# A graph network on one NeuronCore: first products before the second graph's inputs, a re-listed last chain, the last output block through SBUF

## The chip, the cores and the metric

The kernel runs on one core of a Trainium2 chip. The time is what the device measures for one launch, in microseconds (us); of several runs the median counts. All arithmetic is in float32. TensorE (PE) multiplies matrices, VectorE (DVE), ScalarE (ACT) and GpSimd (POOL) do the elementwise work, and SyncE (SP) issues the transfers between the chip's memory and the on-chip memory SBUF. Matrix products land in PSUM, which here is used as eight banks of 128 x 512 numbers.

## What is computed

There are 64 graphs of 256 nodes with 512 features each, and one adjacency matrix `adj` (256 x 256) for all. Two layers follow each other, both with a residual connection. The normalisation has no learned scale.

```python
h = relu(layernorm(x))                                  # layer 0: attention with a mask
q, k, v = h @ Wq + bq, h @ Wk + bk, h @ Wv + bv         # 8 heads of 64
p = softmax(q @ k.T / 8 + (1 - adj) * -1e9)             # per graph and head
x = x + (p @ v) @ Wo + bo

h = relu(layernorm(x))                                  # layer 1: graph attention
g = h @ W
s1, s2 = g @ a1, g @ a2
e = leaky_relu(s1[:, None] + s2[None, :], 0.2) * adj
x = x + elu(softmax(e) @ g + beta * g)
```

## The kernel before

**Pairs and seven products.** The graphs are worked off in 32 pairs. For a pair, the activations form a 2 x 2 matrix of blocks: the rows are the two graphs, the columns the two halves of 256 features. Each weight matrix is split 2 x 2 as well. A product of the two is then made with seven block products in place of eight. This needs four sums of blocks on each side ahead of the products and seven sums of results behind them. `Unit.p(i)` (L261-275) issues product i, where i is 1 to 7; each product is eight matmuls of 128 x 256. `UnitQK` makes q and k (two units, `ua` and `ub`, of one 128-column tile each), `UnitV`, `UnitO` and `UnitW` make v, the output projection and the second layer's product. Products 1 and 2 need only original blocks, products 5 to 7 and 3 need sums. The activation's sums are `combine_31` (L281), `combine_2` and `combine_4` (L291, L295). Weight sums are made once by `weight()` (L101-121). The sums of results are in the `put...` functions of each unit: `put11` after product 2, `put2` (`put2_sums` and `put2_elu` in `UnitW`) after product 5, `put12` after product 3. The block that a product writes into is taken from eight PSUM banks in turn, and the elementwise tiles from pools with a fixed number of buffers per tag (`set`, `qk`, `v`, `pt`, `xt`, ...).

**Layer 0.** `load(p)` (L76) fetches x of a pair. `stats` and `scales` (L231-248) make mean and reciprocal deviation on DVE and POOL. ACT normalises x in place, `x_t` (L307) transposes it on TensorE and ACT applies relu (h). `combine_31` of h reads the transposes of the second graph straight from PSUM. `scores` (L396) makes q.k, exp on ACT and the mask on POOL; `values` (L425) makes p.v, and the division on DVE gives `oT`. `o_blocks` (L439) forms the first two sums of oT on POOL. `residual` (L449) loads x once more and adds the bias on POOL.

**Layer 1.** `normal` (L490) makes the normalised h of this layer on ACT; `node_sums` (L493, called by `y_sums`) makes s1 and s2 as weighted row sums on DVE (tile `pr`). `gat_scores` (L499) spreads s2 along the rows with two small transposes (tile `pe`) and makes e on DVE, `gat_exp` the exponential on ACT, `gat_divide` (L515) the division with beta added on DVE, `gat_t` (L523) the transposes (tile `at`) and an ACT copy (`eT`). `z_graph` (L532) multiplies h by that, 16 matmuls a graph (tile `pz`), and copies the result with ACT to `z`. `UnitW` (L560) is the last product; `elu` (L566) makes relu and exp of the negative part on ACT and max(x, 0) + y on DVE, `finish` (L575) adds both on POOL and issues the output transfer. For the very last block `put12_finish` (L601) does this in two halves of 256 columns.

**Order.** The order of the instructions on TensorE, DVE, ACT and POOL is the order in which the Python code issues them (`tc.manual_schedule`, L969). Each of these engines works its list off from front to back; an instruction whose inputs are not there holds up all behind it. SP's list of transfers is arranged by the framework. `start()` (L675) is the beginning of the first pair, the loop body is `first_half` and `second_half`, which interleave the two layers of neighbouring pairs, `last()` (L859) is the last pair's layer 0, and `end()` (L910) the second layer of the last two pairs, 60/61 and 62/63. Behind `end()` comes a check (L991-1003) that the softmax sums lie in a safe range: seven small DVE operations, a matmul `count`, and a flag. The flag decides whether a second, slower version of the program has to be run; SP loads it and branches.

Of the kernel before, what the change touches and what calls it, by code (L numbers as in the profile page):

```python
# [23 lines left out]
def kernel(ctx: ExitStack, tc: tile.TileContext, x, adj, wq, bq, wk, bk, wv, bv, wo, bo, w, a, beta, out):  # L24
# [42 lines left out]
    def two(ps):  # L67
        return ps.rearrange("p (j n) -> p j n", j=2)
# [7 lines left out]
    def load(p):  # L76
        for g in (2 * p, 2 * p + 1):
            for t in range(NT):
                XT[g, t] = sb([P, D], "xt", f"x_{g}_{t}", BUFS["xt"])
                nc.sync.dma_start(XT[g, t], x[g, t * P:(t + 1) * P, :])  # L80

    load(0)
# [18 lines left out]
    def weight(name, src, permuted=False):  # L101

        raw = const.tile([P, 3, 2, N], F32, name=f"{name}_b")
        b12 = blk("set", f"{name}_b12")
        tt = const.tile([P, 4, 2, N], F32, name=f"{name}_t")
        for dst, r, f in ((raw[:, 0], 0, 0), (raw[:, 1], 1, 0), (b12, 0, 1), (raw[:, 2], 1, 1)):
            if permuted:
                for i in range(4):
                    nc.sync.dma_start(dst[i * HH:(i + 1) * HH], wo_rows(src)[r, i, :, :, f * N:(f + 1) * N])
            else:  # L110
                nc.sync.dma_start(dst, rows_in_order(src)[r, :, :, f * N:(f + 1) * N])
        b11, b21, b22 = (raw[:, i] for i in range(3))
        t1, t2, t3, t4 = (tt[:, i] for i in range(4))

        def sums():
            nc.vector.tensor_tensor(t1, b12, b11, ALU.subtract)
            nc.vector.tensor_tensor(t2, b22, t1, ALU.subtract)
            nc.vector.tensor_tensor(t3, b12, b22, ALU.subtract)
            nc.vector.tensor_tensor(t4, b21, t2, ALU.subtract)

        return {1: b11, 2: b21, 3: b22, 4: t4, 5: t1, 6: t2, 7: t3}, b12, sums
# [7 lines left out]
    WQ, _, wq_sums = weight("wq", wq)  # L129
    WK, _, wk_sums = weight("wk", wk)  # L130
# [4 lines left out]
    WV, _, wv_sums = weight("wv", wv)  # L135
# [26 lines left out]
    def project_b():  # L162


        WO, b12, sums = weight("wo", wo, True)
        nc.sync.dma_start(bo2, bo.partition_broadcast(P))
        bvc = sb([P, DC], "bvc", "bvc", 1)
        with nc.allow_non_contiguous_dma(reason="a bias, once"):
            bv_v = bv.rearrange("(q i s d) -> i d q s", q=2, i=4, s=2, d=HH)
            for i in range(4):  # L170
                for q in range(2):
                    nc.sync.dma_start(bvc[i * HH:(i + 1) * HH, 2 * q:2 * q + 2], bv_v[i, :, q, :])
        cbs = []

        def part(n):
            if n == 0:
                sums()
            elif n == 1:
                for c in range(DC):
                    if c % 2 == 0:  # L180
                        cbs.append(sb([P, 2, P], "rec", f"bvb_{c}"))
                    nc.vector.tensor_scalar(cbs[-1][:, c % 2, :], ones, bvc[:, c:c + 1], None, ALU.mult)
            else:
                ps = bank("pbo")
                for c in range(DC):
                    for f in range(2):
                        b = ((WO[1], b12), (WO[2], WO[3]))[c // 2][f]
                        nc.tensor.matmul(ps[:, f * N:(f + 1) * N], cbs[c // 2][:, c % 2, :], b[:, c % 2, :],
                                         start=(c == 0 and f == 0), stop=(c == DC - 1), skip_group_check=True)
                nc.vector.scalar_tensor_tensor(bo2, bo2, -1.0, ps, op0=ALU.add, op1=ALU.add)  # L190

        return WO, part

    def project_a():

        blocks_w, b12, sums = weight("w", w)
# [110 lines left out]
    def x_t(p):  # L307

        s = blocks(("h", p), f"h{p}")
        pss = {}  # L310
        for gi in range(2):
            g = 2 * p + gi
            for half in range(2):
                ps = pss[gi, half] = bank(f"tr_{g}_{half}")
                for c in range(2):
                    for t in range(NT):
                        f0 = (2 * half + c) * P
                        nc.tensor.transpose(ps[:, c * N + t * P:c * N + (t + 1) * P], XT[g, t][:, f0:f0 + P], ident)
                dst = blk("set", f"h_{g}_{half}")
                nc.scalar.activation(dst, two(ps), AF.Relu)  # L320
                s[BLOCK[2 * gi + half]] = dst

        def relu_of(ps):
            return lambda dst, op, other: nc.vector.scalar_tensor_tensor(dst, two(ps), 0.0, other, op0=ALU.max, op1=op)

        combine_31(s, relu_of(pss[1, 0]), relu_of(pss[1, 1]))
        for g in (2 * p, 2 * p + 1):
            for t in range(NT):
                XT.pop((g, t))
# [230 lines left out]
    class UnitW(Unit):  # L560
# [5 lines left out]
        def elu(self, gi, fh, src, o=None):  # L566
            g = 2 * self.pair + gi
            m = blk(self.tags[0] if (gi, fh) != (0, 0) else "m", f"m_{g}_{fh}")
            nc.scalar.activation(m, src, AF.Relu, scale=-1.0)
            nc.scalar.activation(m, m, AF.Exp, scale=-1.0)  # L570
            o = o or blk(self.tags[1], f"o_{g}_{fh}")
            nc.vector.scalar_tensor_tensor(o, src, 0.0, Y.pop((g, fh)), op0=ALU.max, op1=ALU.add)
            self.o[gi, fh] = (o, m)
# [19 lines left out]
        def put2_elu(self):  # L593
            self.elu(1, 1, self.c, self.c)
            self.elu(1, 0, two(self.d))
# [5 lines left out]
        def put12_finish(self):  # L601

            g = 2 * self.pair
            y, m, o = Y.pop((g, 1)), blk("pt", f"m_{g}_1"), blk("pt", f"o_{g}_1")
            for t in range(NT):
                src = self.b[:, t * N:(t + 1) * N]
                nc.vector.tensor_tensor(src, src, self.u2[:, t, :], ALU.add)
                nc.scalar.activation(m[:, t, :], src, AF.Relu, scale=-1.0)
                nc.scalar.activation(m[:, t, :], m[:, t, :], AF.Exp, scale=-1.0)
                nc.vector.scalar_tensor_tensor(o[:, t, :], src, 0.0, y[:, t, :], op0=ALU.max, op1=ALU.add)  # L610
            for t in range(NT):
                nc.vector.tensor_tensor(o[:, t, :], o[:, t, :], m[:, t, :], ALU.add)
# [61 lines left out]

    def start():  # L675
# [3 lines left out]
        for g in range(2):  # L679
# [4 lines left out]
            for t in range(NT):  # L684
                nc.scalar.activation(XT[g, t], XT[g, t], AF.Identity, bias=nmr[:, t:t + 1], scale=rstd[:, t:t + 1])
        wq_sums()
        x_t(0)
# [4 lines left out]
        ua, ub, uv = UnitQK(0, 0), UnitQK(0, 1), UnitV(0)  # L692
        ua.p(1)
        ub.p(1)
# [12 lines left out]
        shift(0)  # L707
# [5 lines left out]
        scores(0, 0)  # L713
        products(uv, 4, 6)
# [144 lines left out]
    def last(uv):  # L859
# [28 lines left out]
        residual(p, 1, 1, "qk")  # L888
# [5 lines left out]
        o_blocks(p)  # L894
        residual(p, 1, 0, "qk")
        residual(p, 0, 1, "qk")
        add()
        uw.put2_elu()
        uw.p(3)
        uo = UnitO(p)  # L900
        products(uo, 1, 4)
        combine_2(A["o", p])
        uw.put12()
        combine_4(A["o", p])
# [3 lines left out]
        return uo  # L908

    def end(uo):  # L910
        p = NP - 1
        g0, g1 = 2 * p, 2 * p + 1
        products(uo, 6)
        y_sums(p - 1, 0, 0, 1)
        products(uo, 2)
        gat_scores(g0 - 2)
        gat_exp(g0 - 2)
# [13 lines left out]
        z_graph(p - 1, 0)  # L931
        normal(g0, rstd, minus(mr, f"y{g0}"), "qk")
        z_graph(p - 1, 1)
# [8 lines left out]
        combine_4(z)  # L942
        y_sums(p, 0, 0, 1)
        products(uw, 6, 2)
        gat_divide(ATT[g1], gsums[:, NT * g1:NT * g1 + NT], g1)
        products(uw, 7)
        gat_scores(g0)
        gat_exp(g0)
        products(uw, 5)
        uw.finish(0, 0, nc.gpsimd)  # L950
        gat_t(g1)
        gat_divide(ATT[g0], gsums[:, NT * g0:NT * g0 + NT], g0)
        uw.finish(1, 1, nc.gpsimd)
        uw.p(3)
        gat_t(g0)
        uw.put12()
        uw.finish(1, 0, nc.gpsimd)
        uw.finish(0, 1, nc.gpsimd)
        gat_z(p)
        combine_24(A["z", p])  # L960
        uw = UnitW(p, ("pt", "xt"))
        products(uw, 1, 4, 6, 2, 7, 5)
        uw.finish(0, 0, nc.gpsimd)
        uw.finish(1, 1, nc.gpsimd)
        uw.p(3)
        uw.put12_finish()
        uw.finish(1, 0, nc.gpsimd)

    with tc.manual_schedule(engines={ENG.PE, ENG.DVE, ENG.Activation, ENG.Pool}):  # L969
# [6 lines left out]
        end(last(uv))  # L976
# [13 lines left out]

    bad = sb([P, 3], "bad", "bad", 1)  # L991
    for j, (src, op, bound) in enumerate(((acc, ALU.is_le, SAFE), (gsums, ALU.is_le, SAFE),
                                          (gsums, ALU.is_ge, 1.0 / SAFE))):
        ok = sb([P, N], "rec", f"ok_{j}")
        nc.vector.tensor_scalar(ok[:, :src.shape[-1]], src, bound, None, op)
        nc.vector.tensor_reduce(bad[:, j:j + 1], ok[:, :src.shape[-1]], AX.X, ALU.min)
    nc.vector.tensor_scalar(bad, bad, -1.0, 1.0, ALU.mult, ALU.add)
    ps = bank("count")
    nc.tensor.matmul(ps[:1, :3], ones[:, :1], bad, start=True, stop=True)
    count = const.tile([1, 1], F32, name="count_f")  # L1000
    nc.vector.tensor_reduce(count, ps[:1, :3], AX.X, ALU.add)
    flag = const.tile([1, 1], I32, name="flag")
    nc.vector.tensor_copy(flag, count)
# [150 lines left out]
```

## Time and profile before

| | before |
|---|---|
| median of 3 runs | 2868.06 us (2867.16 to 2870.11) |
| profiled execution | 2870.91 us, its span 2869.1 us |
| mean granted TensorE clock | 0.995 |
| TensorE busy | 2842.2 us, 99% |
| VectorE busy | 2064.7 us, 72% |
| ScalarE busy | 1047.0 us, 36% |
| GpSimd busy | 1624.0 us, 57% |
| moved by DMA | 110.00 MB, mean 38 GB/s |

The profile is one execution on the core, taken by the hardware profiler. A row of the timeline reads: start, duration, engine, line of the kernel's file, operation, output and inputs by the program's names, and in brackets how long the engine had been idle before it and who ended that. A row of waits reads: engine, what waited, who released it, total us, number of times, longest. "Clock" is the share of its full clock that TensorE was granted. The chain that ended last is not resolved in this profile, so the argument rests on waits, windows and the timeline.

### The profile page before, as it was taken

The page shows a single profiled execution, that of the slowest core. Times are in us where ns is not written, and L with a number is a line of the kernel's source. Part 1 is how long each engine was busy: PE and PEld are TensorE (multiplying, and loading weights), DVE is VectorE, ACT ScalarE, POOL GpSimd, SP SyncE. Part 2 cuts the span into 40 slices and gives each one's busy share as a digit, 9 for nine tenths or more (in the row PEclk, how much of TensorE's full clock was granted, in tenths as well). Part 3 has the DMA queues.
Part 4 walks back from the last instruction along what each step waited for, and adds up shares of the span by engine and source line. Part 5 has one row for each costly group of instructions (what it writes and reads, how often), then busy time and mean ns, then how long its engine had stood idle before and what let it go on. Part 6 is the DMA issues. An engine that isn't in the chain of part 4 may idle for free.

```text
span 2869.1 us, 46358 instructions
## 1 busy us (share of the span) xinstructions
PE 2842.2 (99%) x18110; PEld 2332.9 (81%) x18110; DVE 2064.7 (72%) x3651; ACT 1047.0 (36%) x2118; POOL 1624.0 (57%) x1592
## 2 busy tenths in 40 slices
PE   9999999999999999999999999999999999999997
PEld 7788888888888888888888888888888888888876
DVE  5766776767867677767677676786767776767866
ACT  2233433333433334333343333343333433333433
POOL 3755655556555556555565555655555655556581
PEclk9999999999999999999999999999999999999998
DMA  5000111101111001110011110011100111001101
GB/s 155 23 27 19 45 45 45 34 19 38 45 45 45 17 29 45 45 45 30 16 45 45 45 44 15 31 45 45 45 20 26 45 45 45 30 23 38 33 23 35
DMA packets 96479, 110.00 MB, mean 38 GB/s; under 512 B 8576, under 2 KB 79488, under 8 KB 96256
## 3 DMA queue, kind: packets, MB, share of 16 engines
q1 hardware_dynamic: 96256, 106.99, 11.9%
q8 instruction: 145, 2.38, 0.4%
q14 instruction: 78, 0.64, 0.1%
HBM read 73.41 MB, written 33.55 MB: 37 GB/s over the span
## 4 chain that ended last, share of the span: by engine, by line


## 5 line engine op out<-in xcount | busy, mean ns | idle before, releaser
L408 POOL TENSOR_TENSOR pt<-pt,maskT 128x512 f32<-128x512 f32 x512 | 719.6, 1405 | 554.3 <-ACT pt L407 554.3
L410 POOL TENSOR_TENSOR pp<-pt 128x256 f32<-128x256 f32 x512 | 432.6, 845 | 40.1
L407 ACT ACTIVATE pt<-sc 128x512 f32<-128x512 f32 x512 | 264.6, 602 | 339.0 <-PE sc L403 332.7
L578 POOL TENSOR_TENSOR o<-o,m 128x512 f32<-128x512 f32 x40 | 51.1, 1281 | 516.6 <-ACT m L570 477.9
L496 DVE SCALAR_TENSOR_TENSOR pr<-h,war 128x512 f32<-128x512 f32 x256 | 300.8, 1218 | 57.4 <-ACT h L490 57.4
L403 PE MATMUL sc<-qk 64*128 64x256 f32 x2048 | 255.7, 389 | 0.0
L421 PE MATMUL av<-pt,v 128*32 128x256 f32 x4096 | 247.6, 382 | 0.0
L403 PEld LDWEIGHTS sc<-qk 64*128 64x128 f32 x2048 | 187.3, 186 | 69.7 <-PE av L421 38.3
L542 PE MATMUL pz<-eT,h 128*128 128x256 f32 x1024 | 228.6, 382 | 0.7 <-ACT eT L530 0.7
L432 DVE RECIPROCAL rec<-sm 128x256 f32<-128x256 f32 x128 | 223.3, 1745 | 3.5 <-PE sm L430 3.5
L542 PEld LDWEIGHTS pz<-eT,h 128*128 128x128 f32 x1024 | 196.1, 192 | 28.2 <-ACT eT L530 1.1
L421 PEld LDWEIGHTS av<-pt,v 128*32 128x32 f32 x4096 | 120.0, 109 | 108.4 <-issue 31.8
L339 PE MATMUL qk_p<-s_h,wq_t 128*128 128x256 f32 x768 | 197.5, 379 | 0.0
L339 PE MATMUL qk_p<-s_h,wk_t 128*128 128x256 f32 x768 | 197.1, 379 | 0.0
L372 PE MATMUL o_p<-wo_t,s_o 128*128 128x256 f32 x768 | 178.9, 383 | 1.9 <-DVE s_o L291 1.9
L372 PE MATMUL w_p<-w_t,s_z 128*128 128x256 f32 x768 | 176.5, 379 | 0.0
L372 PE MATMUL v_p<-wv_t,s_h 128*128 128x256 f32 x768 | 176.3, 379 | 0.0
L556 DVE TENSOR_TENSOR s_z<-pz,z 128x512 f32<-128x512 f32 x64 | 44.2, 691 | 172.6 <-ACT z L545 172.6
L372 PEld LDWEIGHTS o_p<-wo_t,s_o 128*128 128x128 f32 x768 | 147.3, 192 | 23.2 <-issue 2.2
L545 ACT COPY z<-pz 128x512 f32<-128x512 f32 x128 | 74.9, 586 | 244.8 <-PE pz L542 244.8
L372 PEld LDWEIGHTS v_p<-wv_t,s_h 128*128 128x128 f32 x768 | 145.8, 190 | 20.1 <-ACT pt L407 0.3
L339 PEld LDWEIGHTS qk_p<-s_h,wk_t 128*128 128x128 f32 x768 | 145.9, 190 | 19.8
(172 smaller groups left out, 5721.1 us busy)
## 6 DMA issues: line engine op xcount, KB each, us to landing
x<-in_x_dram SPq DMA_DIRECT2D x128, 256.0 KB, 3.5
y<-in_x_dram SPq DMA_DIRECT2D x128, 256.0 KB, 2.8
out_dram<-o SPq DMA_DIRECT2D x127, 256.0 KB, 2.2
wq_b<-in_L_gnn_Wq_dram SPq DMA_DIRECT2D x4, 256.0 KB, 6.2
wk_b<-in_L_gnn_Wk_dram SPq DMA_DIRECT2D x4, 256.0 KB, 6.5
wv_b<-in_L_gnn_Wv_dram SPq DMA_DIRECT2D x4, 256.0 KB, 4.7
wo_b<-in_L_gnn_Wo_dram SPq DMA_DIRECT2D x16, 64.0 KB, 2.3
w_b<-in_L_gnn_W_dram SPq DMA_DIRECT2D x4, 256.0 KB, 3.4
```

Source lines behind the costliest of these rows:

```text
L339: nc.tensor.matmul(ps[:, j * N:(j + 1) * N], wj[i][:, c, ft * P:(ft + 1) * P], s[i][:, c, :], start=(start and j == 0 and c == 0), stop=(c ...
L372: nc.tensor.matmul(ps[:, t * N:(t + 1) * N], s[i][:, c, t * P:(t + 1) * P], wj[i][:, c, :], start=(start and t == 0 and c == 0), stop=(c = ...
L403: nc.tensor.matmul(pss[2 * pair + h][:, k * N:(k + 1) * N], qk[hs, 1, k * P:(k + 1) * P], qk[hs, 0, :], start=True, stop=True)
L407: nc.scalar.activation(pt, two(pss[i]), AF.Exp, scale=QSCALE)
L408: nc.gpsimd.tensor_tensor(pt, pt, maskT, ALU.mult)
L410: nc.gpsimd.tensor_tensor(pp, pt[:, 0, :], pt[:, 1, :], ALU.add)
L421: nc.tensor.matmul(ps[i * HH:(i + 1) * HH, s * N:(s + 1) * N], v[:, k, c0:c0 + HH], pts[i][:, k, :], start=(k == 0), stop=(k == NT - 1))
L432: nc.vector.reciprocal(rec, sums[:, :N])
L496: nc.vector.scalar_tensor_tensor(pr, H2[g][t], 1.0, war[:, j, :], op0=ALU.mult, op1=ALU.mult, accum_out=SC[g][:, t, j:j + 1])
L542: nc.tensor.matmul(ps[:, f * N:(f + 1) * N], h2[k][:, fs], eT[:, k, :], start=(k == 0), stop=(k == NT - 1))
L545: nc.scalar.copy(dst, two(ps))
L578: eng.tensor_tensor(o, o, m, ALU.add)
```

## The change

It has three parts; the number of matrix products stays the same.

1. *Start.* `load` takes the graphs to be loaded, and `weight` hands out a function that fetches chosen quarters. The transfers are listed as x of graph 0, first quarters of Wq and Wk, x of graph 1, then the other quarters of Wq and Wk in turn. `x_t` is split into `x_t_graph` and `x_31`. `start()` normalises and transposes graph 0, issues product 1 of both units, and then transposes graph 1. The sums for Wo (`shift(0)`) move from before the mask's copies to behind `scores(0, 0)`.
2. *Last chain.* In `last()` and `end()` the sums, copies and additions of the last two pairs are listed in another order: row sums of graph 60 between the sums of o; product 2 of o before 6; `put2_elu` and `put12` of pair 58/59 later; the second graph of pair 60/61 multiplied right behind the first; of pair 62/63, `z_graph` of graph 63 before product 3 of the pair before, that of graph 62 behind it; the products of the last unit as 1, 4, 6, 7, 5, 2, 3; the range check and its count matmul moved forward into `end()`.
3. *Last block.* `put12_finish` writes its sum to SBUF (`v`) instead of PSUM and takes exp of it directly; the minimum with 1 is taken by the last DVE operation. This is one ACT operation per half instead of two.

```diff
-    load(0)
+    load(0, 0)
...
+    wq_fetch(0)
+    wk_fetch(0)
+    load(0, 1)
+    for j in range(1, 4):
+        wq_fetch(j)
+        wk_fetch(j)
...
-            src = self.b[:, t * N:(t + 1) * N]
-            nc.vector.tensor_tensor(src, src, self.u2[:, t, :], ALU.add)
-            nc.scalar.activation(m[:, t, :], src, AF.Relu, scale=-1.0)
-            nc.scalar.activation(m[:, t, :], m[:, t, :], AF.Exp, scale=-1.0)
-            nc.vector.scalar_tensor_tensor(o[:, t, :], src, 0.0, y[:, t, :], op0=ALU.max, op1=ALU.add)
+            nc.vector.tensor_tensor(v[:, t, :], self.b[:, t * N:(t + 1) * N], self.u2[:, t, :], ALU.add)
+            nc.scalar.activation(m[:, t, :], v[:, t, :], AF.Exp)
         for t in range(NT):
-            nc.vector.tensor_tensor(o[:, t, :], o[:, t, :], m[:, t, :], ALU.add)
+            nc.vector.scalar_tensor_tensor(o[:, t, :], v[:, t, :], 0.0, y[:, t, :], op0=ALU.max, op1=ALU.add)
+        for t in range(NT):
+            nc.vector.scalar_tensor_tensor(o[:, t, :], m[:, t, :], 1.0, o[:, t, :], op0=ALU.min, op1=ALU.add)
             nc.sync.dma_start(out[g, t * P:(t + 1) * P, N:], o[:, t, :])
...
@@ start()
+        normals(0)
+        x_t_graph(0, 0)
+        normals(1)
+        ua, ub, uv = UnitQK(0, 0), UnitQK(0, 1), UnitV(0)
+        ua.p(1)
         wq_sums()
-        x_t(0)
+        ub.p(1)
+        x_t_graph(0, 1)
+        x_31(0)
         wk_sums()
         combine_24(A["h", 0])
         load(1)
         wo_blocks, shift = project_b()
-        ua, ub, uv = UnitQK(0, 0), UnitQK(0, 1), UnitV(0)
-        ua.p(1)
-        ub.p(1)
         products(ua, 2)
...
         products(ub, 6)
-        shift(0)
         masks(m)
...
         scores(0, 0)
+        shift(0)
         products(uv, 4, 6)
...
@@ last()
         uo = UnitO(p)
-        products(uo, 1, 4)
-        combine_2(A["o", p])
+        uo.p(1)
+        uo.p(4)
+        y_sums(p - 1, 0, 0)
+        combine_24(A["o", p])
+        y_sums(p - 1, 0, 1)
...
@@ end()
-        products(uo, 6)
-        y_sums(p - 1, 0, 0, 1)
         products(uo, 2)
         gat_scores(g0 - 2)
         gat_exp(g0 - 2)
+        uo.p(6)
+        uw.put2_elu(True)
+        uw.put12()
...
         z_graph(p - 1, 0)
+        z_graph(p - 1, 1)
         normal(g0, rstd, minus(mr, f"y{g0}"), "qk")
-        z_graph(p - 1, 1)
...
-        products(uw, 5)
-        uw.finish(0, 0, nc.gpsimd)
+        uw.p(7)
         gat_t(g1)
+        uw.put11()
+        uw.p(5)
+        uw.put2_sums()
+        combine_4(z)
+        uw.finish(0, 0, nc.gpsimd)
+        z_graph(p, 1)
         gat_divide(ATT[g0], gsums[:, NT * g0:NT * g0 + NT], g0)
-        uw.finish(1, 1, nc.gpsimd)
+        uw.put2_elu()
         uw.p(3)
         gat_t(g0)
         uw.put12()
+        uw.finish(1, 1, nc.gpsimd)
         uw.finish(1, 0, nc.gpsimd)
         uw.finish(0, 1, nc.gpsimd)
-        gat_z(p)
+        bad = in_range()
+        ps = A["z", p]["ps"]
+        z_graph(p, 0)
+        A["z", p]["ps"] = ps
+        z_31(p)
         combine_24(A["z", p])
         uw = UnitW(p, ("pt", "xt"))
-        products(uw, 1, 4, 6, 2, 7, 5)
-        uw.finish(0, 0, nc.gpsimd)
-        uw.finish(1, 1, nc.gpsimd)
+        uw.p(1)
+        uw.p(4)
+        uw.p(6)
+        uw.p(7)
+        uw.p(5)
+        uw.put2_sums()
+        uw.p(2)
+        uw.put2_elu()
+        uw.put11()
+        uw.finish(1, 1, nc.gpsimd)
+        uw.finish(1, 0, nc.gpsimd)
+        uw.finish(0, 0, nc.gpsimd)
+        count(bad)
         uw.p(3)
         uw.put12_finish()
-        uw.finish(1, 0, nc.gpsimd)
```

## The prediction

> **What bounds the kernel now.** I read the page first (whose busy time fills the span), then TensorE's waits (where it does not work), then a table of windows (where those waits lie, and at which clock), and then the timeline of the two ends.
>
> ```profile
> span 2869.1 us, 46358 instructions
> ...
> PE 2842.2 (99%) x18110; PEld 2332.9 (81%) x18110; DVE 2064.7 (72%) x3651; ACT 1047.0 (36%) x2118; POOL 1624.0 (57%) x1592
> ```
>
> The span is a TensorE span: 99% busy, VectorE only 72%. Nothing shortens it but fewer matmuls (the change keeps their number) or less time in which TensorE waits or runs slowly.
>
> ```profile
> PE pe L160 <- DVE pr L496: 4.2, 2, 3.5
> PE w_p L372 <- DVE o L590: 2.8, 2, 2.1
> PE tr L318 <- ACT x L685: 2.8, 4, 1.9
> PE o_p L372 <- DVE s_o L291: 1.9, 1, 1.9
> PE qk_p L339 <- DVE qk L357: 1.6, 1, 1.6
> PE at L529 <- DVE e L520: 1.5, 1, 1.5
> ...
> PE w_p L372 <- ACT z L545: 1.3, 1, 1.3
> PE pz L542 <- ACT eT L530: 0.7, 1, 0.7
> ```
>
> Each wait occurs once or a few times in 64 graphs: these are the prologue (L318, L339) and the last chain (the rest), not the loop.
>
> ```profile
> 15.00:30.00 15.00, 15.00 (x68) 13.02 (x67) 8.56 (x16) 3.37 (x7) 0.00 (x0) 0.96 0.68 189
> ...
> 100.00:2600.00 2500.00, 2500.00 (x16031) 2055.62 (x16030) 1807.20 (x3181) 924.49 (x1867) 1436.04 (x1398) 1.00 0.12 37
> ...
> 2784.40:2860.40 76.00, 63.58 (x268) 51.41 (x264) 53.59 (x108) 26.43 (x57) 23.15 (x23) 0.89 0.09 31
> 2860.40:2869.10 8.70, 0.00 (x0) 0.00 (x0) 2.83 (x7) 2.02 (x5) 2.06 (x2) 0.64 0.29 97
> ```
>
> Columns: window, length, then TensorE, its weight loads, DVE, ACT, POOL busy, granted clock. From 100 to 2600 us TensorE is busy for 2500.00 of 2500.00 at clock 1.00. The stretch from 2784.4 to its last matmul (2860.4) has 63.58 busy of 76.00 at clock 0.89; then 8.7 us follow without matmuls. So there are about 40 us in front and 85 behind to argue about.
>
> **Head.** First matmul groups of before (start, duration, engine):
>
> ```profile
> 8.23 0.98 PE L318 MATMUL tr<-ident,x 128*128 128x128 f32 x7 [0.38 <-ACT x L685]
> ...
> 11.07 0.33 PE L318 MATMUL tr<-ident,x 128*128 128x128 f32 x1 [1.86 <-ACT x L685]
> ...
> 12.59 1.75 PE L339 MATMUL qk_p<-h,wq_b 128*128 128x256 f32 x4
> ...
> 17.74 1.03 PE L339 MATMUL qk_p<-h,wq_b 128*128 128x256 f32 x4
> ...
> 40.67 1.13 PE L339 MATMUL qk_p<-s_h,wq_b 128*128 128x256 f32 x4 [1.56 <-DVE qk L357]
> ```
>
> Graph 0 is transposed by 9.21; graph 1's transposes run 11.07-12.76; the two p1 products follow, until 16.16 at half clock: four matmuls in 1.75 against 1.03. Afterwards p1 of both units needs only graph 0, so it goes between the two sets of transposes. It needs wq[0] and wk[0]. SP now issues 2 x loads, wq[0], wk[0], 2 x loads, then weights in turn. The four x loads took 1.81 us to issue and landed 3.4-7.1; wq[0] landed 5.8 us after its issue at 2.59. Issued about 1 us sooner, wq[0] lands near 7.0-7.5 and wk[0] by 8.3 (the 256-KB pieces landed 0.75 us apart). h of graph 0 (two relus of 0.5) is done near 9.5: p1 of both runs 9.55-13.0 (2 x 1.73). x of graph 1 lands 8-9, behind two weight pieces (7.0 before). Its statistics, POOL's three operations and the ACT normals took 4.7 us from landing to end (7.01-11.72), so normals end near 12.5-13.2. Transposes take 1.1 us: 13.0-14.1. The p2 products end at 17.55; in before their end, the start of p4, was 21.19. Gain 3.65, of which 1.7 is the half-clock spell.
>
> Against it: wk's four VectorE sums queue behind wq's and behind x_31, wq[3] lands later, and ub.p4 waits about 0.65 (0-1.1). The four wo sums (35.83-38.43, 2.7 us) move from before the mask copies to after ub's last sum. There they took VectorE while L357 was wanted; the 1.56 wait at 40.67 goes. In the new place VectorE idled 4.77 us at 48.35: cover for 2.7, also if contended (4.5). Gone, that cover would cost up to 1.8. Behind the moved loads on SP, the four wo pieces that slip between the two x pairs of load(1) (0.63 each to issue) delay x by 2.5 us; x_stats need it some 10 us after landing: nothing. Head: 3.65 - 0.65 + 1.56 = **4.5 us** (3.2 to 5.5).
>
> **Last chain.** Times in before's clock from 2784.42, where uw.p3 starts. TensorE's work to the end, at full clock: 22 products x 1.725 = 37.95, two sets of 32 pz matmuls x 6.9 = 13.8, small transposes about 4.3: 56 of 76.0. The other 20 are waits (12.4, the waits above) and half clock (2798.0-2804.9 and 2832.2-2842.4).
>
> Walk of the new order: p3, p1, p4, p2 to 2791.4. Then pe of graph 60 waits for y_sums, now among the s_o sums on DVE. From 2787.1: pr twice 1.2, s_o 1.74 and 1.6, pr 1.2 and 0.65: 2794.6, an idle of 3.15 (before 3.47+0.69 here and 1.88 for s_o). p6, p7, p5 to 2800.05. at(61) waits for the divide: idle 2.05, done 2803.9. p3 and 32 pz to 2812.5 (pz began at 2809.13). pe(63): idle 0.7. Products p1, p4 without the 1.28 for z; p6 with 0.25; p2, pe, p7, at, p5, then graph 63's 16 pz, which fill the 2.10 that p3 waited for L590, then p3, at(62): 2831.5. Then the other 16 pz wait for eT of 62: its ACT copy is queued behind one z copy and four ELU operations (0.6 each): idle 1.5. pz to 2836.45, seven products to **2848.5**: the last p3 has two products behind what it waits for, so the 0.72 at 2858.40 goes.
>
> Half clock on top: +1.3 (0 to 3.4). Here row and rule differ.
>
> ```profile
> 2828.80:2832.20 3.40, 1.30 (x8) 0.99 (x7) 3.34 (x9) 1.51 (x6) 0.00 (x0) 1.00 0.21 75
> 2832.20:2842.40 10.20, 7.98 (x20) 5.42 (x20) 5.09 (x10) 4.44 (x8) 3.76 (x3) 0.50 0.22 77
> ```
>
> Row: a window of 3.4 us with 1.30 busy, its longest gap 2.10, was followed by clock 0.50, as was 9.33-12.75 (1.30 busy, gap 1.86). The Trainium skill, TensorE: Matmul & The Clock Gate, "HAM oscillation": only gaps over about 3.4 us bring the throttle back. By it the 3.15 costs 0; by the rows it brings one spell, 1.7 at most, less what at(61) waits anyway. I take the rows.
>
> For the s_o stretch: a DVE sum of two SBUF inputs took 1.74 beside a POOL add and 0.69 alone:
>
> ```profile
> 2789.79 2.94 POOL L453 TENSOR_TENSOR y<-y,bo 128x512 f32<-128x512 f32 x2
> 2789.86 1.74 DVE L291 TENSOR_TENSOR s_o<-s_o,oT 128x512 f32<-128x512 f32 x1 [0.56 <-POOL s_o L445]
> ...
> 2820.44 0.69 DVE L291 TENSOR_TENSOR s_z<-s_z,z 128x512 f32<-128x512 f32 x1
> ```
>
> The skill's SBUF — State Buffer, "SBUF: two separate sides", says the loser waits for the whole other instruction. This speaks against sums placed there: with strict turns between POOL's six adds of up to 1.47 (2784.4-2793.6) and DVE, pe comes at 2795.6 and the idle is 4.15. The rows give 3.15, which I take, and keep 2.2-4.2. POOL's bias add of y(1,1), moved behind the s_o sums, is first wanted at 2799.90: nothing.
>
> Moved at no cost: the range check (seven small DVE operations, about 2.8 us) lies under graph 62's pz, where DVE idled 7.16 before 2846.13; without that cover it costs 2.8. put2's ELU on DVE, put12 and combine_4 run under the next products.
>
> Drain: last matmul to last DVE was 3.9 (two serial rounds of add, relu, exp, max). Now the sum goes to SBUF; exp needs no relu ahead of it (one ACT operation of 0.42 per half instead of two) and DVE's six operations of 0.42 run nearly on end: 3.2. SP's load of the flag stands before the last outputs: 0-0.8, taken 0.4 (in before under 1.45 and hidden). Last DVE to end stays 4.8. 8.7 becomes 8.4.
>
> Sum behind: 76.0 + 8.7 = 84.7 becomes 64.1 + 1.3 + 8.4 = 73.8: **-10.9** (-8 to -13.5).
>
> **Sum.** -15.4 on the profiled execution (2870.91, span 2869.1 and 1.8 outside): 2855.5. It stands 2.85 over the median 2868.06, so the forecast is **2852.7**.
>
> **Rivals.**
> 1. The head's gain is lost on DMA. For: DMA engines are busy to 0.90 in the first 15 us, and the 1-KB pieces of weights share them with x. If graph 1's x lands at 11.4 (wk[0]'s 6.8 from its issue at 4.6), its transposes start at 14.8; the idle of 1.8 brings half clock (1.7) and p2 ends near 21.0. Against: x landed 3-4.5 us from issue. Time: only the tail, 2868.06 - 10.9 = 2857.2.
> 2. The tail's waits come back: DVE in strict turns (+1.0), ACT's ELU ahead of eT(62) at 3 instead of 1.5, at(61) at 3.5 instead of 2.05, a second spell (+1.7): 5.7 less gain, 2858.4. For: 53.6 of DVE work lie on this stretch of 64. Against: DVE waited for others in most of the second half.
> 3. No effect: what is saved at the pe waits is paid again at the next product, because the DVE chain behind y_sums keeps its length; and the head as in 1. Gain under 5.7: about 2864. Against: the seven products and pz that now fill waits are independent of that chain.
> 4. Slower: TensorE's clock. If gaps of 1.4 us or more stay in every 3.4-us window of the last chain, it runs at half clock throughout; each such window loses up to 1.7 us. 15.4 + 5.7 us are gone from 13 windows on, of 19 in 64 us. At 16 windows: 2868.06 - 15.4 + 27 = 2879.7. For: half-clock spells did last two and three windows. Against: windows of 57-61% busy kept full clock, and my walk has six gaps in all.
>
> **How the numbers follow.** A measurement of this kernel can tell about 0.2% (5.7 us) from nothing. Forecast (head 3.2-5.5, tail 8-13.5): 0.72, its own range 2849-2857. Rival 1: 0.10; rival 2: 0.12; rival 3: 0.04; rival 4: 0.02. Faster: the first three, 0.94; same 0.04; slower 0.02. The range 2848.5-2858.8 holds the forecast and the likelier part of rivals 1 and 2; the rest above it is under 2 in 10.
>
> **What would show it.** Right: ua.p1 near 9.6 us ahead of graph 1's transposes; no 0.50 clock at 12.75; no wait of qk_p for L357's line; the last chain's product time from uw.p3 to last matmul 64-66 us; waits of pe for pr near 3, of pz for eT near 1.5; last matmul to end near 8.4. Wrong: transposes of graph 1 after 14.5, ub.p4 waiting over 1.1, more than two half-clock windows behind 2784, or any wait in the loop between 60 and 2740 us, where nothing moves.

## The result and the profile after

The changed kernel takes 2855.87 us (median of 6 runs, 2854.6 to 2857.51) against 2867.61 us for the kernel before (median of 6, 2866.34 to 2870.11). The ratio is 0.9959, 95% interval 0.9946 to 0.9971: 11.7 us less (8 to 15). The forecast was 2852.7, with 2848.5 to 2858.8 as range: the sign and the range held, the gain was 3.2 us smaller than the number.

The page of the changed kernel, span and busy times:

```profile
span 2855.7 us, 46364 instructions
...
PE 2837.8 (99%) x18110; PEld 2331.3 (82%) x18110; DVE 2067.1 (72%) x3651; ACT 1045.4 (37%) x2116; POOL 1624.5 (57%) x1592
```

The number of matmuls is the same, 18110. TensorE's busy time fell by 4.4 us all the same, since fewer of them ran at half clock: the start had 3.4 us of it and has none, and in the last chain 17.1 us became 10.2. Its waits, in total, number and longest:

```profile
PE pe L171 <- DVE pr L513: 4.0, 1, 4.0
PE at L546 <- DVE e L537: 1.6, 1, 1.6
...
PE pz L559 <- ACT eT L547: 1.3, 1, 1.3
PE tr L331 <- ACT x L725: 0.4, 1, 0.4
PE w_p L389 <- DVE s_z L304: 0.3, 1, 0.3
PE qk_p L356 <- ACT h L333: 0.2, 1, 0.2
```

The waits for L590, for L291's s_o, for z and for L357's qk are gone, as is most of the wait of the transposes. What stays is one large wait, pe for pr, larger than before (3.99 against 3.47). The start, in the timeline:

```profile
9.64 1.13 PE L356 MATMUL qk_p<-h,wq_b 128*128 128x256 f32 x4 [0.25 <-ACT h L333]
...
13.20 1.04 PE L331 MATMUL tr<-ident,x 128*128 128x128 f32 x8
...
17.52 1.03 PE L356 MATMUL qk_p<-h,wq_t 128*128 128x256 f32 x4
```

Product 1 begins at 9.64, graph 1's transposes at 13.20, product 4 at 17.52. The last chain, cut where the clock changes (window, length, then TensorE, weight loads, DVE, ACT, POOL busy, granted clock, and the DMA engines' busy share and GB/s):

```profile
2779.20:2788.80 9.60, 7.28 (x37) 6.13 (x33) 9.41 (x10) 2.66 (x5) 9.22 (x8) 1.00 0.08 27
2788.80:2795.63 6.83, 5.16 (x13) 4.17 (x14) 4.98 (x11) 0.91 (x4) 1.06 (x1) 0.50 0.00 0
2795.63:2802.45 6.82, 4.96 (x24) 3.45 (x23) 5.92 (x13) 2.23 (x4) 3.76 (x3) 1.00 0.32 115
2802.45:2805.87 3.42, 3.42 (x10) 2.71 (x9) 3.32 (x10) 0.17 (x1) 0.03 (x1) 0.50 0.00 0
2805.87:2847.44 41.57, 39.99 (x190) 34.04 (x188) 30.16 (x66) 20.12 (x43) 9.66 (x12) 1.00 0.07 26
```

Two stretches ran at clock 0.50, with 8.58 us of busy time for 23 matmuls; the 24 matmuls at 2838.33, at full clock, took 5.34. Behind 2805.87 the chain is nearly tight: 39.99 of 41.57 busy. The steps of the prediction beside the two profiles (us):

| | before | foretold | after |
|---|---|---|---|
| product 4 begins | 21.19 | 17.55 | 17.52 |
| product 4's Wk half waits | none | 0.65 | 0.1 |
| product 3 of the second unit waits | 1.56 | 0 | 0 |
| uw.p3 begins | 2784.42 | 4.5 earlier | 2779.20, 5.2 earlier |
| uw.p3 to last matmul | 75.97 | 65.4 | 68.24 |
| of this, TensorE idle | 12.4 | 7.65 | 7.43 |
| last matmul to end | 8.71 | 8.4 | 8.26 |
| span | 2869.1 | 2853.7 | 2855.7 |

### The profile page after: what moved, and what is told of

It reads as the page before. It is cut to its first block, busy times and chain, and to the rows that moved or that the text cites. A ratio compares the mean times of both kernels' runs of the same rounds, so it can differ in the third digit from the quotient of the medians.

```text
span 2855.7 us, 46364 instructions
## 1 busy us (share of the span) xinstructions
PE 2837.8 (99%) x18110; PEld 2331.3 (82%) x18110; DVE 2067.1 (72%) x3651; ACT 1045.4 (37%) x2116; POOL 1624.5 (57%) x1592
## 5 line engine op out<-in xcount | busy, mean ns | idle before, releaser
L389 PEld LDWEIGHTS w_p<-w_t,s_z 128*128 128x128 f32 x768 | 145.6, 190 | 20.3 <-issue 0.6
```

The source lines that it names most:

```text
L389: nc.tensor.matmul(ps[:, t * N:(t + 1) * N], s[i][:, c, t * P:(t + 1) * P], wj[i][:, c, :], start=(start and t == 0 and c == 0), stop=(c = ...
```

## Experiments: which part gives what

**E1, the start alone.** The kernel before with the change's `load`, `weight`, `x_t_graph` and `start()`; `last()`, `end()` and the last block as before.

> The change's start on the kernel before, its last chain and last block as before. Theory (the parts add up): the start gains what the profile of the changed kernel shows there, 3.7 us until product 4 of the first unit and 1.6 us at product 3 of the second, so 5.2 us less than before (ratio 0.998). Rival 1: the DMA order costs again later what it gave (pair 1's x behind Wo), gain under 3 us. Rival 2: start and end interact through the phase of the clock's windows, so that the parts do not add up to the whole by over 2 us.

Measured: 2865.78 us (13 runs) against 2867.82 (18 runs), ratio 0.9992 (0.9984 to 1.0): 2.0 us less, not 5.2. Its one profiled execution (2861.07, the fastest of the 13) shows the start as the changed kernel has it (product 4 at 17.36, uw.p3 at 2779.16), so the position is right and the size in the medians is not. Rival 1 said under 3 us, but its mechanism, transfers that come late later, shows nowhere: uw.p3 is as early as in the changed kernel. What rival 2 names, the phase of the clock, is at work, but between one profile and the medians; the parts themselves add up, as E2 shows. In this profile the last chain, in the order of before, took 71.50 us, where the profile of before has 75.97. The first two lines are from before, the last two from E1:

```profile
2800.30 5.88 PE L372 MATMUL o_p<-wo_t,s_o 128*128 128x256 f32 x16
...
2837.74 9.46 PE L542 MATMUL pz<-eT,h 128*128 128x256 f32 x32 [0.68 <-ACT eT L530]
```

```profile
2794.95 3.63 PE L389 MATMUL o_p<-wo_t,s_o 128*128 128x256 f32 x16
...
2830.30 7.17 PE L559 MATMUL pz<-eT,h 128*128 128x256 f32 x32 [0.68 <-ACT eT L547]
```

These two groups alone account for the 4.5 us. In E1 the half clock (2787.1-2790.5 and 2824.6-2828.0) fell on products after which TensorE waited anyway. The median of E1 leaves about 76.2 us for the same chain (2865.78 less the 1.8 outside the span, the 2779.16 and the 8.64 behind the last matmul; an estimate, if those two stay), so 75.97 seems to be the usual case and 71.50 the rare one.

**E2, the end alone.** The changed kernel with `start()` and the transfers of before.

> The change's last chain and last block with the start of before. Theory: 8 us less than before (7.8 from the last chain, 0.4 behind the last matmul; ratio 0.9971). Rival: the last chain was worth the predicted 10.9 and something in the start ate 3 us of it: then 11 us less here (0.9962).

Measured: 2858.37 against 2867.82, ratio 0.9966 (0.9954 to 0.9978): 9.5 us less, between the two expectations. 2.0 + 9.5 = 11.5 is the whole (11.7): the parts add up. What the two missed is seen in the timeline of this run's start, which has the order of before:

```profile
9.95 0.33 PE L327 MATMUL tr<-ident,x 128*128 128x128 f32 x1 [0.53 <-ACT x L720]
...
11.48 1.03 PE L352 MATMUL qk_p<-h,wq_b 128*128 128x256 f32 x4
...
18.39 1.03 PE L352 MATMUL qk_p<-h,wq_t 128*128 128x256 f32 x4
```

The same instructions in the same order as in the profile of before, yet product 4 begins at 18.39 and not at 21.19. Graph 1's transposes began 1.1 us sooner, and the four matmuls of product 1 took 1.03 instead of 1.75. The profile of before had drawn a late x and a half-clock stretch of 3.4 us at 12.75. Its mean clock was 0.995; 57 later runs of before have 0.996 to 0.998. Against this start the change gains 0.9 us at product 4, and 2.4 at uw.p3 (2781.62 to 2779.20), which agrees with the 2.0 of E1 and with 2858.37 - 2855.87 = 2.5. Those later runs carry no timeline, so that the typical start of before looks like E2's is inferred from these agreements.

**E5, the sums for Wo back.**

```diff
         products(ub, 6)
+        shift(0)
         masks(m)
...
         scores(0, 0)
-        shift(0)
```

> The changed kernel with the four sums for Wo back in front of the mask's copies. Theory (they held up the q and k results that product 3 of the second unit waits for): a wait of about 1.6 us of TensorE at that product comes back, the first score product starts at about 38.8 in place of 37.15, and the time rises by 1.6 us (ratio to before 0.9965 in place of 0.9959). Rival: with product 4 earlier by 3.7 us DVE has slack, the sums hide, under 0.5 us.

```profile
PE qk_p L356 <- DVE qk L374: 1.6, 1, 1.6
```

The wait is back, the first score product begins at 38.92 in place of 37.15, and the time is 2857.89, ratio 0.9967 (0.9954 to 0.9981), 2.0 above the changed kernel (the intervals overlap; the trace is what shows it). So of the 2.4 us of the start, about 1.7 are this one move of four DVE sums, and the new order of the first products is worth under 1 us on a start like E2's.

**E6, the transfers back.** The changed kernel with `load(0)`, all of Wq, all of Wk, in this order; the order on the engines stays.

> The changed kernel with the transfers of the start in the order of before (x of both graphs, all of Wq, all of Wk); the order on the engines stays changed. Theory (the new order serves to have the first quarter of Wk there when product 1 wants it): the first product's Wk half waits until about 10.5 to 11.4 us, product 4 begins about 1 us later (18.5 in place of 17.5), 1 us more. Rival: the transfers need no new order, since x of graph 1 then lands earlier and what product 1 loses the transposes win: within 0.3 us.

```profile
9.45 1.13 PE L352 MATMUL qk_p<-h,wq_b 128*128 128x256 f32 x4 [0.25 <-ACT h L329]
10.71 1.13 PE L352 MATMUL qk_p<-h,wk_b 128*128 128x256 f32 x4
```

Wk's half of product 1 begins 0.1 us later than in the changed kernel (10.61), product 4 at 17.73 (0.2 later); 2856.48, ratio 0.9961 (0.9946 to 0.9976). By the trace the rival is right, the new order of the transfers is hardly needed: uw.p3 begins 0.2 later too (2779.39). The medians, 0.6 apart, cannot tell 0.2 from 1.

## Experiments: the large wait and the half clock

**E3, POOL's additions away.** `residual(p, 1, 1)`, `(1, 0)` and `(0, 1)` of the last pair without the addition on POOL (`bias=False`), so the bias is missing from these three blocks:

```diff
-        nc.gpsimd.tensor_tensor(r, r, bo2[:, fh * N:(fh + 1) * N].unsqueeze(1).to_broadcast([P, 2, N]), ALU.add)
+        if bias:
+            nc.gpsimd.tensor_tensor(r, r, bo2[:, fh * N:(fh + 1) * N].unsqueeze(1).to_broadcast([P, 2, N]), ALU.add)
```

> The changed kernel; the addition of the output bias to three blocks of the last pair, on POOL, is left out (its y comes straight from the transfer). Theory (DVE's sums with two SBUF inputs wait for POOL's additions): pr and s_o fall from 1.2-1.75 us to 0.7 once POOL's s_o sums are done, the pe wait of 3.99 falls below 1, the half clock behind it goes, and uw.p3 to last matmul falls from 68.2 to about 62: 5 to 6.5 us less than the changed kernel (ratio to before about 0.994). Rival 1 (pe waits for the number of DVE operations ahead of it, not for POOL): the wait stays above 2.5 and the time falls by under 2 us. Rival 2 (the wait moves on to at, behind the divide): pe wait goes, at's wait grows from 1.65 to over 4, time falls by about 2.

The DVE operations ahead of pe, first in the changed kernel, then in E3 (start, duration):

```profile
2784.20 1.74 DVE L304 TENSOR_TENSOR s_o<-s_o,oT 128x512 f32<-128x512 f32 x1
2785.97 1.64 DVE L308 TENSOR_TENSOR s_o<-oT,s_o 128x512 f32<-128x512 f32 x1
2787.53 1.75 DVE L513 SCALAR_TENSOR_TENSOR pr<-h,war 128x512 f32<-128x512 f32 x1
...
2789.21 1.20 DVE L513 SCALAR_TENSOR_TENSOR pr<-h,war 128x512 f32<-128x512 f32 x1
```

```profile
2784.11 1.21 DVE L304 TENSOR_TENSOR s_o<-s_o,oT 128x512 f32<-128x512 f32 x1
2785.35 0.69 DVE L308 TENSOR_TENSOR s_o<-oT,s_o 128x512 f32<-128x512 f32 x1
2785.96 0.68 DVE L514 SCALAR_TENSOR_TENSOR pr<-h,war 128x512 f32<-128x512 f32 x1
...
2786.57 0.68 DVE L514 SCALAR_TENSOR_TENSOR pr<-h,war 128x512 f32<-128x512 f32 x1
```

Without POOL beside it, a DVE operation with two SBUF inputs takes 0.68 here; beside its additions of 128x512 it takes 1.64 to 1.75. The two of 1.20 and 1.21 overlap POOL's work in part. The wait of pe falls from 3.99 to 0.9, the chain from 68.24 to 62.65, the time to 2850.96, ratio 0.994 (0.9927 to 0.9954): 4.9 less than the changed kernel, 5 to 6.5 expected. Part of it went where rival 2 pointed: at's wait grew from 1.6 to 2.3, and one stretch at half clock is left (2795.7-2799.1).

**E4, fill the wait.** 20 transposes of the identity into unused columns of the pe bank, ahead of pe of graph 60.

> The changed kernel with 20 transposes of the identity (about 2.2 us at full clock) into an unused part of the pe bank, while TensorE waits for pr. Their results are not read. Theory (the clock is halved by a window in which TensorE is mostly idle): products 6, 7, 5 take 5.4 us in place of 7.76; pe comes no sooner; at's divide comes up to 1 us sooner; total 1.5 to 3 us less than the changed kernel. Rival (the half clock has another cause): 7.7 us as before, and no gain.

```profile
2790.49 0.32 PE L171 MATMUL pe<-ident,s 128*128 128x128 f32 x1 [1.82 <-DVE pr L513]
2790.65 5.35 PE L389 MATMUL o_p<-wo_t,s_o 128*128 128x256 f32 x24
...
2798.34 2.19 PE L548 MATMUL at<-ident,e 128*128 128x128 f32 x8 [2.33 <-DVE e L539]
```

pe comes at the same moment (2790.49 against 2790.47), and the 24 matmuls behind it take 5.35 us; in the changed kernel they took 7.76. at begins 1.8 us sooner. The phase of the clock's windows differs between the two profiles, but four other profiles with the unfilled wait (E2, E5, E6, E8) also have 6.72 to 7.71 for these matmuls. The cause of this stretch at half clock was TensorE's idleness, nothing in the products; another stretch still follows at's wait (2798.2-2801.6). The chain is 65.38 in place of 68.24; the medians show 1.0 us of it (2854.85, ratio 0.9953, 0.994 to 0.9967), which does not stand clear of the changed kernel.

**E8, eT of graph 62 ahead of the ELU.**

```diff
-        uw.put2_elu()
         uw.p(3)
         gat_t(g0)
+        uw.put2_elu()
```

> The changed kernel with the ACT copy of eT of graph 62 listed ahead of the four ELU operations of blocks (1,1) and (1,0) of pair 60/61 (and their two DVE additions behind it). Theory (the 1.3 us wait of pz is ACT's queue): the wait falls to about 0.6, the time of one transpose and one copy, and the total by 0.7 us. Rival: the ELU then delays the additions on DVE and with them z's sums, the wait moves to w_p, no gain.

```profile
PE w_p L389 <- ACT z L562: 1.1, 1, 1.1
PE pz L559 <- ACT eT L547: 0.7, 1, 0.7
```

pz's wait falls to 0.7 as expected, and a new one of 1.1 stands at the next unit's first product, which needs a copy of z: the ELU now delays z's copies on ACT. 2857.52, ratio 0.9965 (0.9952 to 0.9978). The rival is right. ACT has the same ELU operations to do before z's copies, and in this order either eT or z pays.

## Experiments: a shorter last chain

E3 and E4 say that the chain is bound by what TensorE's order puts behind a late row sum. Four more orders of the same instructions were tried, all on the changed kernel.

**E7.** pe of graph 60 behind products 6 and 7; graph 61's division and transposes before the s_o sums; graph 61's pz behind product 5.

```diff
         products(uo, 2)
+        products(uo, 6, 7)
         gat_scores(g0 - 2)
         gat_exp(g0 - 2)
-        uo.p(6)
...
-        products(uo, 7)
-        divide(p - 1)
-        products(uo, 5)
+        uo.p(5)
+        uo.put2_k()
+        z_graph(p - 1, 1)
```

> The changed kernel with a last chain in which pe of graph 60 stands behind products 6 and 7 of o, the division of graph 61 is made before the s_o sums, graph 61's 16 pz matmuls stand behind product 5, graph 60's behind product 3, product 1 of the next unit before pe of graph 63, and the ELU of pair 58/59 on DVE behind the statistics. Theory (TensorE waits in the last chain because its next work stands behind a short transpose whose DVE chain is late, and the half clock follows from those waits): the wait of pe falls from 4 us below 1, no half clock before 2805, uw.p3 to last matmul falls from 68.2 to 59-63 us, 5 to 9 us less than the changed kernel (ratio to before 0.993). Rival (VectorE, some 55 us busy in this stretch, is the bound behind it): waits of w_p for s_z and of pz for eT take the place, gain of 0 to 3 us.

Graph 60's pz began at 2799.47 and was through at 2803.1, where the changed kernel had both graphs' pz done only at 2812.65. Then all of it was lost:

```profile
PE w_p L389 <- ACT z L567: 4.4, 1, 4.4
```

z's copies of graph 60 stood on ACT behind graph 63's normalisation and an ELU that waited for DVE. Half clock followed (2805.4-2812). 2857.61, ratio 0.9967 (0.9955 to 0.998): no gain. Neither theory nor rival: it was ACT's queue, not DVE's load.

**E9.** E7's order, with z's copies of graph 60 ahead of the normalisation, the ELU of pair 58/59 behind graph 62's scores, product 7 ahead of pe of graph 62, and E8's edit.

> As e7, and: the copies of z of graph 60 stand on ACT ahead of graph 63's normalisation, the DVE and ACT part of the ELU of pair 58/59 stands behind the scores of graph 62, product 7 ahead of pe of graph 62, and eT of 62 ahead of the ELU. Theory (e7 won 9.7 us up to the end of graph 60's pz and lost them in one wait, w_p for a copy of z that stood behind other work on ACT): the 4.4 wait and its half clock go, uw.p3 to last matmul 59-63 us, 5 to 9 us less than the changed kernel (ratio to before 0.993). Rival (VectorE is the bound behind it): the wait comes back at pe or at of graphs 62 and 63, over 3 us, gain under 3 us.

The chain is 64.75, no stretch of it runs at half clock, and all five runs lie within 0.2 us: 2853.94 (2853.88 to 2854.08), ratio 0.9952 (0.9938 to 0.9966), 1.9 less than the changed kernel, not the 5 to 9 expected. No wait is over 1.2 us; several of 0.7 to 1.2 are left, two of them for z and for one DVE sum.

**E10.** E9's order, with eT behind the ELU again, product 3's sums and graph 62's division ahead of the rest of the old ELU on DVE.

> As e9, with eT of graph 62 behind the ELU on ACT again (as in the changed kernel), and on DVE the sums that product 3 needs and the division of graph 62 ahead of the rest of the ELU of pair 58/59. Theory (e8 and e9 show that z's copies may not stand behind the ELU, and that product 3 waited 1.2 us for one sum): w_p's waits for s_z and for z go, pz waits about 1.3 once; the last chain takes 62.5-64 us in place of 64.75, 1 to 2 us less than e9. Rival (DVE is the bound from graph 63's sums on): the wait goes to at or pz, within 0.5 us of e9.

```profile
PE pz L564 <- ACT eT L552: 4.4, 2, 3.8
```

2856.25, ratio 0.996 (0.9947 to 0.9974). Not expected by either theory: the old ELU's two ACT operations waited for DVE ahead of z's copies, and eT with them. The wait of 3.8 brought half clock (2826.3-2833.1), in which the 16 pz took 6.57 us in place of 3.72.

**E11.** E10's order, with eT ahead of the ELU, and the two ELU blocks that nobody waits for behind the last z copies and sums, beside the last unit's products.

```diff
+        uw.p(1)
+        uw.p(4)
+        for late in (old, prev):
+            late.put12()
+            late.finish(0, 1, nc.gpsimd)
+        uw.p(6)
```

> As e10, and: eT of graph 62 ahead of the ELU of blocks (1,1) and (1,0), and the last ELU of pairs 58/59 and 60/61 behind the z copies and sums of graph 62, beside the last unit's products. Theory (what is left in the last chain are copies that TensorE needs and that stand behind ELU work that nobody waits for): the wait of pz for eT of 62 falls from 3.8 to 0.7, w_p's wait for z stays away, no half clock, uw.p3 to last matmul about 61.5 us (e9: 64.75), total about 2851 us, 3 us less than e9. Rival (DVE, with two ELU blocks moved behind the sums, delays the last unit's sums): wait of the last product 3 or of z's sums over 1.5 us, no better than e9.

```profile
PE pe L171 <- DVE pr L518: 1.5, 2, 0.9
...
PE at L551 <- DVE e L542: 1.0, 1, 1.0
...
PE pz L564 <- ACT eT L552: 0.7, 1, 0.7
```

The chain is 62.03, pz's wait 0.7, w_p waits for nothing. 2851.88 us (2851.29 to 2852.18), ratio 0.9943 (0.9929 to 0.9957): 15.8 less than before and 4.0 less than the changed kernel, with the same work. One stretch at half clock remained in its profile (2814.6-2818.0), where the expectation had none.

## Why the prediction was right, and where it was off

The number is 3.2 us too low: the span 2.0 (the last chain 2.8 more than foretold, the start 0.7 and the end 0.1 less), and 1.2 from the profile's distance to the median. No term has the wrong direction. In medians it looks different. Of the 4.5 us foretold for the start (3.2 to 5.5) E1 found 2.0, with an interval of 0 to 4.6, and the comparison with E2's start 2.4; of the 10.9 for the end (8 to 13.5) E2 found 9.5. The largest miss is thus most likely the size of the start.

Of the signs named ahead, product 1 at 9.6, full clock at 12.75, no wait for L357's line, pz for eT near 1.5 and the end near 8.4 came. The last chain (68.24, not 64 to 66) and the wait of pe (3.99, not near 3) did not, and one sign of being wrong did: three windows at half clock behind 2784, where more than two were to count against it.

*Half clock in the last chain* (foretold +1.3, at most 3.4). The idle time came out as walked, 7.43 us against 7.65, but partly by luck: the wait of pe was 0.84 longer than taken, that of at 0.4 shorter, and the 0.7 before graph 63's pe did not occur. What failed is the price of the idle time. By rows of the same matmuls at full clock, the two stretches cost 7.76 - 5.34 on products 6, 7, 5, 3.43 - 1.89 on product 3, and 7.37 - 7.07 on pz: 4.3 us. The prediction counted one stretch and reckoned that the wait of at would absorb part of it. The first lasted two windows instead of one, since the wait reached into the next window; the second followed at's wait. These 3.0 us are the chain's excess of 2.8. E4 shows that they hang on the idleness: filled, the first stretch goes. The 4.3 is one draw too. E2, E5 and E6 have the same last chain, and there both stretches are one window long and cost 2.4 to 3.1 us by the same rows of products, for chains of 67.2 to 67.6.

*From the profile to the median* (taken as 2.85). The changed kernel's profile stands only 1.64 over its median: 1.2 us. Behind this lies the step "It stands 2.85 over the median 2868.06, so the forecast is 2852.7": it took the distance as something that stays. But 2.8 us of the start of before, a late x and a half-clock stretch, belonged, as far as E2 shows (18.39 against 21.19), to that one execution. The step "Gain 3.65, of which 1.7 is the half-clock spell" removed a cost that the typical run most likely does not have. From profile to profile the start gained 5.2; E1's and E2's medians say 2.0 to 2.5.

*Right:* the start's walk (product 4 at 17.52, foretold 17.55) and the wait of product 3, which E5 brings back by putting the four sums back. The cover named for the sums' new place held: no wait appears behind `scores(0, 0)`. There the sums took 4.2 us, as the 4.5 allowed for contention had it. The new wait of pz for eT was 1.3 (foretold 1.5), w_p's for s_z 0.26 (0.25).

*The end behind the last matmul* (8.26, foretold 8.4) agrees because two errors cancel. The last DVE operation came 3.65 after the last matmul and not 3.2 (before: 3.90), since the two maxima took 1.41 beside POOL's additions; from there to the end it took 4.6, where 4.8 and 0.4 for the flag had been taken. This rest is unsteady: with the same last block, E2 to E6 have 7.6 to 8.2 in all. By the DVE operations the last block through SBUF is worth about 0.25 us (3.90 in E1 as well, 3.65 or 3.66 in E2 to E4).

*The rule against the row.* For the s_o stretch the prediction took 2794.6 from single rows and named 2795.6, an idle of 4.15, by the Trainium skill's rule (SBUF — State Buffer, "SBUF: two separate sides") that the loser waits for the other's whole instruction. Measured: 3.99. The rule was the better guide. E3 shows that POOL's additions are the cause: without them the wait is 0.9. It does not show whether one engine waits for the other's whole instruction or both merely slow each other down.

*Rivals.* Of rival 2, the pe wait longer by 1 us (which it put down to strict turns of DVE and POOL) and the second stretch came, eT and at did not get worse. Rival 1's late x did not come: graph 1's normals were done when TensorE reached their transposes. Rivals 3 and 4 have nothing in the trace.

## What to carry to other kernels

A profile is one draw: before a stall is counted as gain, ask whether a second execution of the same instructions has it (product 4 at 21.19 and 18.39, a last chain of 75.97 and 71.50), and do not carry a profile's excess over the median through as a constant. A short operation whose input is late should stand behind the products that don't need it, and a copy that TensorE needs should not stand on its engine behind work that nobody waits for (E7 and E10 lost 4.4 and 3.8 us that way, E11 won 4.0 by the opposite). A wait of TensorE costs more than its length, since the matmuls behind it may run at half clock.

## What was not expected of the hardware

Within one execution the granted clock changed on a raster of 3.41 us. Between executions the raster is shifted: it changed at 2798.00 in the profile of before and at 2788.80 in that of the changed kernel, 2.7 windows apart. Windows of the changed kernel's last chain:

```profile
2785.39:2788.80 3.41, 1.09 (x6) 0.66 (x4) 3.38 (x3) 0.00 (x0) 3.41 (x3) 1.00 0.00 0
2788.80:2792.21 3.41, 1.74 (x5) 1.47 (x6) 3.38 (x8) 0.00 (x0) 1.06 (x1) 0.50 0.00 0
...
2799.03:2802.45 3.42, 2.09 (x10) 1.27 (x11) 3.28 (x7) 1.00 (x2) 0.69 (x1) 1.00 0.43 153
...
2829.76:2833.17 3.41, 2.09 (x12) 1.65 (x10) 2.19 (x5) 2.70 (x5) 2.60 (x3) 1.00 0.22 77
```

A window with 1.09 us of matmuls was followed by half clock, one with 1.74 at half clock by more of it, and so was one with 2.09 of 3.42 busy, whose longest wait was 1.65 us. The prediction had read 57-61% busy as safe. The last line, from further on in the same execution, was just as busy (2.09) and was followed by full clock. So the busy share is not, or not alone, what is counted; the window at 2799.03 held eight small transposes and few large matmuls, but which measure it is stays open. Nor does one long gap have to be in the window. E11's stretch at half clock followed this one, in which TensorE never waited longer than 0.96 us:

```profile
2811.19:2814.60 3.41, 1.54 (x8) 0.86 (x6) 3.38 (x13) 0.36 (x2) 0.00 (x0) 1.00 0.00 0
```

The Trainium skill (TensorE: Matmul & The Clock Gate, "HAM oscillation") speaks of gaps above about 3.4 us; here the measurements decide.
